# The last group's sums, norm and stores in two sequences, and the group before it at double pace

## The chip, the cores and the metric

The kernel runs on one core of a Trainium2 chip. A core has TensorE (PE in the profile), VectorE (DVE), ScalarE (ACT), GpSimd (POOL) and SyncE (SP), each with an instruction queue of its own that is worked through in order, and 16 DMA engines. The metric is the device time of one execution in microseconds; the figure quoted is the median of the runs.

## The reference, cut

32 sequences of 128 tokens with 128 features pass one decoder layer: causal self-attention (16 heads of 8), attention to a context, and a mixture of 8 experts of which every token uses 2, each followed by a residual and a layer norm.

```python
x = layernorm(x + attn(x, x, x, causal=True), ln1_g, ln1_b)
x = layernorm(x + attn(x, ctx, ctx, causal=False), ln2_g, ln2_b)
# mixture of experts
r = softmax(x @ router_w + router_b)
topw, topi = top_k(r, 2)
topw = softmax(topw)
h = gelu(x @ w1[e] + b1[e])          # for each expert e, 128 -> 512
y = h @ w2[e] + b2[e]                # 512 -> 128
x = layernorm(x + sum(topw[k] * y[topi[k]] for k in (0, 1)), ln3_g, ln3_b)
```

The layer norm is taken over the 128 features: mean, variance, `(x - m) / sqrt(v + 1e-5) * g + b`.

## The kernel before

The batch is worked in 8 groups of `G = 4` sequences, so a group is 512 tokens, held as a tile of 128 partitions by 4 by 128 (partition = token in its sequence). Both attentions of all groups come first, in half slots written out in a table. At their end each group is routed (`route`, `place`): its tokens are scattered, by expert, into rows of a DRAM buffer `xs`, and its residual (with the experts' second bias weighted in) is kept in DRAM as `x2d`.

The experts then run in two phases of four groups each (`PHASES`). A phase has 39 blocks of 128 rows (`NBL`), and each block belongs to one expert. For block i, `Pipeline.run` issues in this order:

- the load of the weights of block i + 4 (`fetch_weights`, SP's queue, 514 KB; five buffers)
- `first_layer(i)`: 4 products of 128x128 into `ph`, and four gelu activations into `h` on ScalarE (L888, L893)
- `second_layer(i - 1)`: 4 products into `po` (L904), a copy `ot<-po` on VectorE (L909), and on GpSimd a memset and an indirect DMA that scatters the 128 rows to `eo` in DRAM (L910, L911)
- in every fourth block `turn`: transposes of the rows of the next four blocks (`px`), their scatter positions (`row`, `to`) and the copy `xT<-px` on VectorE
- `beside(i)`: the hook in which the groups' final sums are advanced.

The program is under a manual schedule: each engine gets its instructions in the order in which the code issues them, and the framework only adds waits on semaphores. An instruction that waits holds up everything behind it on its engine. Scatters, gelus, copies and the final sums therefore share queues in exactly the order of the calls above.

`combine(gr)` is a generator that finishes one group. It loads `acc` (the residual from `x2d`, L977) and `gt` (both expert results of each token from `eo`, 512 KB, L979) on SP's queue, the second after the scatters of the blocks that can hold rows of the group (`needed`: 15, 23, 31 and 39 blocks of the phase). Each later call of `next` does one step:

1. the two loads
2. to 4. nothing (the load is under way)
5. `acc += wts[0] * gt[0]`, four instructions on VectorE (L996)
6. `acc += wts[1] * gt[1]`, four more
7. `bn_stats`, four (L337)
8. `bn_aggr`, four (L340), and on GpSimd `var + eps` and the power -0.5 (L341, L342)
9. a product on VectorE for the bias of the norm (L344)
10. two activations on ScalarE, which apply the norm to a sequence each (L347)
11. the other two, and on VectorE the product with the gain (L1005)
12. the addition of the bias (L1007)
13. the store of the group to the output, on SP's queue (L1009).

`step()` advances the two oldest unfinished groups by one step each, and `beside` calls it once per block. In the second phase group 4 begins in block 19, group 5 in block 27, group 6 in block 35. Group 7 needs all 39 blocks, so it begins after the loop together with what is left of groups 5 and 6. At most two groups are in `sums[:2]`, so group 7's step 1 comes when group 5 has ended. `acc` has two buffers and `gt` shares four buffers (tag `qb`).

Of the kernel before, what the change touches and what calls it, by code (L numbers as in the profile page):

```python
# [8 lines left out]
F32 = mybir.dt.float32  # L9
# [4 lines left out]
AF = mybir.ActivationFunctionType  # L14
ALU = mybir.AluOpType
AX = mybir.AxisListType

P = 128
# [5 lines left out]
G = 4  # L24
PHASES = ((0, 4), (4, 4))
NP = len(PHASES)
# [3 lines left out]
NBL = [NS + n for n in ND]  # L30
# [17 lines left out]
EPS = 1e-05  # L48
# [5 lines left out]
def bc(ap, axis, n):  # L54

    ap = ap.unsqueeze(axis)
    shape = list(ap.shape)
    shape[axis] = n
    return ap.broadcast_to(shape)
# [3 lines left out]
def kernel(  # L63
# [34 lines left out]
    nc = tc.nc  # L98
    B = x.shape[0]
    NG = B // G  # L100
# [6 lines left out]
    small = ctx.enter_context(tc.tile_pool(name="small", bufs=4))  # L107
# [6 lines left out]
    def mm_tile(shape, name, dtype=F32):  # L114
        return ps_mm.tile(shape, dtype, tag="mm", name=name)
# [36 lines left out]
    class Attn:  # L152
# [20 lines left out]
        out=hm4, in_=hm4, pattern=[[-32, RG], [-8, 4]], compare_op=ALU.is_ge,  # L173
# [3 lines left out]
        out=hm4, in_=hm4, pattern=[[32, RG], [8, 4]], compare_op=ALU.is_ge,  # L177
# [7 lines left out]
    def head_bias(a, n):  # L185

        a.bqm = const.tile([P, 4], F32, name=f"bqm{n}")
        nc.vector.tensor_scalar(a.bqm, hmask, a.bq, None, ALU.mult)
# [10 lines left out]
        out=quarter[rows], in_=quarter[rows], pattern=[[32, RG], [-1, P]],  # L199
# [4 lines left out]
        out=causal[rows], in_=causal[rows], pattern=[[32, RG], [-1, P]],  # L204
# [8 lines left out]
    def clean(t):  # L213
# [10 lines left out]
        out=mp4, in_=mp4, pattern=[[-32, RG], [-4, NPART], [-1, 4]], compare_op=ALU.is_equal,  # L224
# [10 lines left out]
    mhalf = const.tile([P, G], F32, name="mhalf")  # L235
# [14 lines left out]
    lng, lnb, lngT, lnbT, later = [], [], [], [], {}  # L250
# [78 lines left out]
    wts = const.tile([P, 2, B], F32, name="wts")  # L329
# [43 lines left out]
    PAIRS = (slice(0, 2), slice(2, 4))  # L373
# [548 lines left out]
    class Pipeline:  # L922
# [29 lines left out]
        def run(self, beside):  # L952

            self.turn()
            before = None
            for j, (k, i) in enumerate(self.all):
                self.weights(j + AHEAD)
                k.first_layer(i)
                if before:
                    before[0].second_layer(before[1])  # L960
                before = k, i
                if i % XB == min(2, k.width(i // XB) - 1):
                    self.turn()
                beside(k.ph, i)
            before[0].second_layer(before[1])


    def needed(n):

        return NS + 2 * G * (n + 1) - 1  # L970

    def combine(gr):

        p = next(p for p, (g0, n) in enumerate(PHASES) if gr.gi < g0 + n)
        first = FREE[p] + 2 * P * G * (gr.gi - PHASES[p][0])
        gr.acc = moe.tile([P, G, P], F32, tag="acc", name=f"acc_{gr.gi}")
        nc.sync.dma_start(out=gr.acc, in_=x2d[gr.gi])  # L977
        gt = act.tile([P, 2, G, 2 * P], F32, tag="qb", name=f"gt_{gr.gi}", bufs=4)[:, 0]
        i = nc.sync.dma_start(  # L979
            out=gt,  # L980
            in_=eo[p][first : first + 2 * P * G, :].rearrange(
                "(p b k) d -> p b (k d)", p=P, k=2
            ),
        )
        n = needed(gr.gi - PHASES[p][0])
        for j in phases[p].done[:n]:
            tc.add_manual_dep(i.ins, j.ins.name, SYNC, reason="results")
        for j in phases[p].done[n:]:
            tc.declare_no_dep(i.ins, j.ins, reason="rows of later groups")
        phases[p].loads.append(i)  # L990
        for _ in range(4):
            yield
        for k in range(2):
            for b in range(G):
                t = G * gr.gi + b
                nc.vector.scalar_tensor_tensor(  # L996
                    gr.acc[:, b, :], gt[:, b, P * k : P * k + P], wts[:, k, t : t + 1],
                    gr.acc[:, b, :], ALU.mult, ALU.add,
                )
            yield  # L1000
        yield from finish(gr)

    def finish(gr):
        yield from normalize(gr.acc, f"m{gr.gi}")
        nc.vector.tensor_tensor(gr.acc, gr.acc, bc(lng[2], 1, G), ALU.mult)  # L1005
        yield
        nc.vector.tensor_tensor(gr.acc, gr.acc, bc(lnb[2], 1, G), ALU.add)  # L1007
        yield
        nc.sync.dma_start(  # L1009
            out=out[G * gr.gi : G * gr.gi + G].rearrange("b p d -> p b d"), in_=gr.acc  # L1010
        )
# [82 lines left out]
    for gi in range(NG):  # L1094
# [37 lines left out]
        ph = phases[next(p for p, (g0, n) in enumerate(PHASES) if gi < g0 + n)]  # L1132
# [31 lines left out]
    def half_slot(h):  # L1164
        t, half = divmod(h, 2)
        if h < 0 and h in table:
            stir(STIR[0] if h == first_half else STIR[1])
        both_scores(unit(t), unit(t - 2), half)
        if half == 0:
            if unit(t - 3):  # L1170
                values(unit(t - 3))
            if unit(t - 1):
                maxima(unit(t - 1))
        else:
            if unit(t):
                split(unit(t))
            if unit(t - 3):
                outputs(unit(t - 3))
        for f, *args in table.pop(h, []):
            f(*args)  # L1180
        if 0 <= h < STIR[2]:
            stir(STIR[1])
# [11 lines left out]
    with tc.manual_schedule():  # L1194
        for h in range(first_half, 5):
            half_slot(h)

        for a, bo, n in ((sa, bo_s, "s"), (ca, bo_c, "c")):
            bvq = setup.tile([P, P], F32, name=f"bvq{n}")
            nc.vector.tensor_copy(bvq, a.bv.broadcast_to([P, P]))  # L1200
            pbv = mm_tile([P, P], f"pbv{n}")
            nc.tensor.matmul(pbv, lhsT=bvq, rhs=a.wo, start=True, stop=True)
            nc.vector.tensor_tensor(bo, bo, pbv, ALU.add)
        head_bias(ca, "c")
        half_slot(5)
        half_slot(6)
        lnb1c = const.tile([P, P], F32, name="lnb1c")
        nc.vector.tensor_tensor(lnb1c, lnb[0], bo_c, ALU.add)
        for h in range(7, start):
            half_slot(h)  # L1210
        left = [start]
        sums = []

        summed = {}
        for p, (g0, n) in enumerate(PHASES):
            for g in range(n):
                i = needed(g) + 4
                key = (p, i) if i < NBL[p] or p == NP - 1 else (p + 1, i - NBL[p])
                summed[key] = groups["c", g0 + g]

        def step():

            for a in sums[:2]:
                if next(a, a) is a:
                    sums.remove(a)

        def beside(ph, i):
            if table or left[0] < 2 * (len(units) + 3):
                half_slot(left[0])
                left[0] += 1  # L1230
            gr = summed.pop((ph.p, i), None)
            if gr:
                sums.append(combine(gr))
            step()

        blocks.run(beside)
        sums.extend(combine(gr) for _, gr in sorted(summed.items()))
        while sums:
            step()

# [40 lines left out]
```

## Time and profile before

| | us |
|---|---|
| median of 3 runs | 656.05 (651.39 to 667.48) |
| the profiled execution | 655.68 |
| its span, first to last instruction | 654.0 |
| TensorE busy in the span | 583.4 |
| VectorE busy | 410.7 |
| ScalarE busy | 404.4 |
| GpSimd busy | 368.6 |
| TensorE busy from 634 us on | 0.0 |

The span runs from the first to the last instruction, so the execution has 1.7 us outside it. A row of the timeline is start, length, engine, line, operation, output<-inputs, shapes, count, and in brackets the idle time of the engine before it with what ended it; "SPq" is SP's queue of issued DMAs. Neighbouring rows of one kind are merged, so a length with a count above one is that of the stretch. Instructions of one engine overlap by some hundredths of a microsecond in such rows. The number of a block is not in the rows; it follows from the order: the copies `ot<-po` of blocks 30 to 38 of the second phase start at 617.44, 621.28, 623.10, 624.88, 627.00, 628.78, 630.57, 632.41 and 633.52.

### The profile page before, as it was taken

How to read it: one execution, taken by the hardware profiler on the slowest of the kernel's cores; microseconds unless marked ns; L12 is line 12 of the kernel's file. 1: busy time of each engine (PE TensorE's matmuls, PEld its weight loads, DVE VectorE, ACT ScalarE, POOL GpSimd, SP SyncE). 2: the span in 40 equal slices, each digit the busy share in tenths (PEclk: the TensorE clock that was granted, in tenths of full speed). 3: DMA queues.
4: the chain of work that ended last, by engine and by line, in shares of the span. 5: the costliest groups of instructions: out<-in, count | busy, mean ns of one | idle time of the engine just before them, and what ended most of it. 6: DMA issues, size and time to landing. Idle time of an engine off the chain costs nothing. (4 is left out here: it accounts for less than half of the span.)

```text
span 654.0 us, 22743 instructions
## 1 busy us (share of the span) xinstructions
PE 583.4 (89%) x9247; PEld 497.4 (76%) x9247; DVE 410.7 (63%) x1327; ACT 404.4 (62%) x919; POOL 368.6 (56%) x749
## 2 busy tenths in 40 slices
PE   8999899999998999999999988988897978999870
PEld 7777787878876777777876866777797878998870
DVE  3345456665667766786787778884867634543563
ACT  4266576787677468667758676645674446665652
POOL 3256465544645557538737525633788885664561
PEclk9599899999999899999999999987999979999995
DMA  6110610832010011001001100422897989999972
GB/s 130 35 35 4 122 43 3 244 136 66 4 34 3 11 47 32 3 7 56 10 20 34 35 4 14 167 71 73 264 285 261 351 306 365 375 344 383 349 254 70
DMA packets 48041, 82.53 MB, mean 126 GB/s; under 512 B 7968, under 2 KB 26464, under 8 KB 47936
## 3 DMA queue, kind: packets, MB, share of 16 engines
q1 hardware_dynamic: 42816, 71.57, 34.3%
q0 software_dynamic: 4544, 9.38, 3.9%
q8 instruction: 72, 1.18, 0.7%
q14 instruction: 33, 0.27, 0.1%
q10 hardware_dynamic: 576, 0.13, 0.1%
HBM read 62.15 MB, written 23.10 MB: 130 GB/s over the span
## 5 line engine op out<-in xcount | busy, mean ns | idle before, releaser
L893 ACT ACTIVATE h<-ph,wd 128x128 f32<-128x128 f32 x312 | 88.7, 369 | 63.3 <-PE ph L888 21.3
L487 DVE TENSOR_REDUCE m_s<-sc_s 128x8 f32<-128x1024 f32 x64 | 78.3, 1223 | 76.6 <-PE sc_s L448 75.6
L499 POOL TENSOR_SCALAR_AFFINE_SELECT pr_s<-pr_s 128x1024 f32<-128x1024 f32 x64 | 69.9, 1092 | 84.4 <-ACT pr_s L495 84.1
L911 POOL DMA_INDIRECT eo<-ot,to x78 | 77.8, 997 | 55.2 <-DVE acc L996 13.5
L495 ACT ACTIVATE pr_c<-st_c 128x1024 f32<-128x1024 f32 x64 | 65.9, 1029 | 60.7 <-PE st_c L460 60.7
L487 DVE TENSOR_REDUCE m_c<-sc_c 128x8 f32<-128x1024 f32 x64 | 78.1, 1220 | 31.0 <-PE sc_c L448 19.5
L888 PE MATMUL ph<-xT,wd 128*128 128x128 f32 x624 | 86.7, 284 | 9.9 <-DMA wd<-wpk 5.2
L495 ACT ACTIVATE pr_s<-st_s 128x1024 f32<-128x1024 f32 x64 | 65.8, 1028 | 42.9 <-PE st_s L460 42.2
L888 PEld LDWEIGHTS ph<-xT,wd 128*128 128x128 f32 x624 | 78.3, 197 | 14.7 <-DMA wd<-wpk 4.1
L904 PE MATMUL po<-wd,h 128*128 128x128 f32 x624 | 84.6, 280 | 4.9 <-ACT h L893 4.9
L904 PEld LDWEIGHTS po<-wd,h 128*128 128x128 f32 x624 | 77.9, 195 | 5.5 <-ACT h L893 5.5
L448 PE MATMUL sc_c<-k_c,qb_c 32*128 32x128 f32 x1024 | 75.5, 286 | 6.7 <-DVE m_c L487 5.1
L448 PE MATMUL sc_s<-k_s,qb_s 32*128 32x128 f32 x1024 | 76.2, 289 | 0.0
L448 PEld LDWEIGHTS sc_c<-k_c,qb_c 32*128 32x128 f32 x1024 | 63.2, 189 | 12.4 <-DVE m_c L487 7.8
L460 PE MATMUL st_c<-qb_c,k_c 32*128 32x128 f32 x1024 | 71.7, 279 | 0.0
L784 POOL DMA_INDIRECT xs<-x,slots x64 | 64.3, 1005 | 12.8 <-issue 12.2
L460 PE MATMUL st_s<-qb_s,k_s 32*128 32x128 f32 x1024 | 71.6, 278 | 0.0
L460 PEld LDWEIGHTS st_s<-qb_s,k_s 32*128 32x128 f32 x1024 | 67.0, 190 | 0.9
L460 PEld LDWEIGHTS st_c<-qb_c,k_c 32*128 32x128 f32 x1024 | 67.3, 191 | 0.2
L448 PEld LDWEIGHTS sc_s<-k_s,qb_s 32*128 32x128 f32 x1024 | 66.9, 198 | 0.3 <-issue 0.2
L909 DVE COPY ot<-po 128x128 f32<-128x128 f32 x78 | 22.5, 290 | 63.8 <-PE po L904 56.7
L442 PE MATMUL sc_s<-causal,quarter 32*128 32x512 bf16 (+3 forms) x512 | 48.4, 309 | 4.2 <-DVE m_s L487 4.0
(247 smaller groups left out, 1202.8 us busy)
## 6 DMA issues: line engine op xcount, KB each, us to landing
wd<-wpk SPq DMA_DIRECT2D x78, 514.0 KB, 5.4
xs<-blank SPq DMA_DIRECT2D x2, 2600.0 KB
xt<-xs SPq DMA_DIRECT2D x20, 260.0 KB, 6.0
wpk<-in_L_xattn_e_w_dram SPq DMA_DIRECT2D x16, 256.0 KB, 9.5
gt<-eo SPq DMA_DIRECT2D x8, 512.0 KB, 7.0
xg<-in_x_dram SPq DMA_DIRECT2D x8, 256.0 KB, 4.8
eg<-in_ctx_dram SPq DMA_DIRECT2D x8, 256.0 KB
x2d<-base SPq DMA_DIRECT2D x8, 256.0 KB
```

What stands on the lines that cost most here:

```text
L442: nc.tensor.matmul(sc[:, i, :, k], lhsT=quarter[rowsof(g), j, :], rhs=bc(causal[rowsof(g), j, k], 1, 4), start=j == 0, stop=False,)
L448: nc.tensor.matmul(sc[:, i, r, :], lhsT=new.group.qb[rowsof(g), new.b, r, :], rhs=new.group.k[rowsof(g), new.b, :], start=not new.masked, ...
L460: nc.tensor.matmul(st[:, i, r, :], lhsT=old.group.k[rowsof(g), old.b, :], rhs=old.group.qb[rowsof(g), old.b, r, :], start=False, stop=r == 3,)
L487: nc.vector.tensor_reduce(new.m[:, 8 * half : 8 * half + 8], sc.rearrange("p i r k -> p (i r) k"), AX.X, ALU.max,)
L495: nc.scalar.activation(old.pr[:, hs, :], st.rearrange("p i r k -> p (i r) k"), AF.Exp, scale=SCALE)
L499: nc.gpsimd.affine_select(out=old.pr[:, hs, :], in_=old.pr[:, hs, :], pattern=[[0, 8], [1, P]], compare_op=ALU.is_ge, fill=0.0, base=0, ch ...
L784: i = nc.gpsimd.indirect_dma_start(out=xs[ph.p][:, :], out_offset=bass.IndirectOffsetOnAxis(ap=slots[:, k, t : t + 1], axis=0), in_=gr.x2[ ...
L888: nc.tensor.matmul(hid[:, c, :], lhsT=w[:, c * P : (c + 1) * P], rhs=self.xT[i // XB][:, i % XB, :], start=True, stop=True,)
L893: nc.scalar.activation(self.h[i][:, c, :], hid[:, c, :], AF.Gelu, bias=w[:, B1 + c : B1 + c + 1])
L904: nc.tensor.matmul(po, lhsT=h[:, c, :], rhs=w[:, W2 + c * P : W2 + (c + 1) * P], start=c == 0, stop=c == NFC - 1,)
L909: nc.vector.tensor_copy(ot, po)
L911: s = nc.gpsimd.indirect_dma_start(out=eo[p][:, :], out_offset=bass.IndirectOffsetOnAxis(ap=self.to[q][:, i % XB : i % XB + 1], axis=0), i ...
```

## The change

In the last eight blocks of the second phase (i from 31 to 38) `beside` calls `step()` twice. Groups 5 and 6 so take two steps per block there: group 5 does steps 5 to 12 in blocks 31 to 34 and stores in block 35 before group 6's loads are issued in the same block; group 6 does steps 1 to 8 in blocks 35 to 38. Group 6's steps 5 and 6 thereby stand between the copies of blocks 36 and 37, its steps 7 and 8 between those of 37 and 38.

After the loop the last group's loads are issued first, then the remaining steps of group 6, then the last group alone. For it `combine` skips the empty steps and calls `last_sums`. That splits the four sequences in two pairs. For each pair VectorE does the sums and statistics sequence by sequence and GpSimd the power; then VectorE's product and ScalarE's activations pair by pair; then gain and bias pair by pair on tiles of 128x256. Each pair has its own store, the first on SP's queue and the second on ScalarE's.

```diff
--- before.py
+++ after.py
@@ -969,6 +969,45 @@
 
         return NS + 2 * G * (n + 1) - 1
 
+    def last_sums(gr, gt):
+
+        rs = [small.tile([P, 2, 2], F32, tag="rs", name=f"rs_l{ab.start}") for ab in PAIRS]
+        for n, ab in enumerate(PAIRS):
+            st = small.tile([P, 2, 6], F32, tag="st", name=f"st_l{n}")
+            mv = small.tile([P, 2, 2], F32, tag="mv", name=f"mv_l{n}")
+            for b in range(2):
+                y, t = gr.acc[:, ab.start + b, :], G * gr.gi + ab.start + b
+                for k in range(2):
+                    nc.vector.scalar_tensor_tensor(
+                        y, gt[:, ab.start + b, P * k : P * k + P], wts[:, k, t : t + 1], y,
+                        ALU.mult, ALU.add,
+                    )
+                nc.vector.bn_stats(st[:, b, :], y)
+            for b in range(2):
+                nc.vector.bn_aggr(mv[:, b, :], st[:, b, :])
+            nc.gpsimd.tensor_scalar(rs[n][:, 0], mv[:, :, 1], EPS, None, ALU.add)
+            nc.gpsimd.tensor_tensor(rs[n][:, 0], rs[n][:, 0], mhalf[:, :2], ALU.pow)
+            rs[n] = rs[n], mv
+        for n, ab in enumerate(PAIRS):
+            r, mv = rs[n]
+            y = gr.acc[:, ab]
+            nc.vector.scalar_tensor_tensor(
+                r[:, 1], mv[:, :, 0], -1.0, r[:, 0], ALU.mult, ALU.mult
+            )
+            for b in range(2):
+                nc.scalar.activation(
+                    y[:, b, :], y[:, b, :], AF.Identity,
+                    bias=r[:, 1, b : b + 1], scale=r[:, 0, b : b + 1],
+                )
+        for n, ab in enumerate(PAIRS):
+            y = gr.acc[:, ab]
+            nc.vector.tensor_tensor(y, y, bc(lng[2], 1, 2), ALU.mult)
+            nc.vector.tensor_tensor(y, y, bc(lnb[2], 1, 2), ALU.add)
+            (nc.sync, nc.scalar)[n].dma_start(
+                out=out[G * gr.gi + ab.start : G * gr.gi + ab.stop].rearrange("b p d -> p b d"),
+                in_=y,
+            )
+
     def combine(gr):
 
         p = next(p for p, (g0, n) in enumerate(PHASES) if gr.gi < g0 + n)
@@ -988,6 +1027,10 @@
         for j in phases[p].done[n:]:
             tc.declare_no_dep(i.ins, j.ins, reason="rows of later groups")
         phases[p].loads.append(i)
+        if gr.gi == NG - 1:
+            yield
+            last_sums(gr, gt)
+            return
         for _ in range(4):
             yield
         for k in range(2):
@@ -1232,9 +1275,16 @@
             if gr:
                 sums.append(combine(gr))
             step()
-
+            if ph.p == NP - 1 and i >= ph_last - 8:
+                step()
+
+        ph_last = NBL[-1]
         blocks.run(beside)
-        sums.extend(combine(gr) for _, gr in sorted(summed.items()))
+        (last,) = (combine(gr) for gr in summed.values())
+        next(last)
+        while sums:
+            step()
+        sums.append(last)
         while sums:
             step()
```

## Prediction

> **What bounds the kernel now.** I read the chain of waits first, from 612 us to the end, because the change only touches what is issued after block 31 of the last phase. Its columns are start, length and what.
>
> ```profile
> 612.15 6.93 DMA wd<-wpk
> ...
> 631.42 2.07 PE po L904 x16
> ...
> 634.44 2.26 DMA eo<-ot,to
> ...
> 636.90 2.69 DMA gt<-eo
> ...
> 649.13 0.70 DVE acc L1005
> 649.84 0.02 issue
> 649.86 0.69 DVE acc L1007
> ```
>
> Until 633.5 TensorE and the weight loads set the pace. Then comes a chain in which nothing overlaps: copy of block 38 (633.52), its scatter (634.44), the load of group 7's rows (636.90), sums, norm, store, end at 654.0. That is 20.5 us, all that the second half of the change can shorten. Next, SP's own timeline, for who loads and stores when:
>
> ```profile
> 625.26 0.43 SPq L977 DMA_DIRECT2D acc<-x2d  x1
> 626.00 0.33 SPq L979 DMA_DIRECT2D gt<-eo  x1
> 633.37 0.39 SPq L1009 DMA_DIRECT2D out_dram<-acc  x1
> 635.72 0.32 SPq L977 DMA_DIRECT2D acc<-x2d  x1
> 636.90 0.32 SPq L979 DMA_DIRECT2D gt<-eo  x1
> 644.68 6.33 SPq L1009 DMA_DIRECT2D out_dram<-acc  x2
> ```
>
> The first two rows are group 6's loads, the third is group 5's store, then group 7's loads, then two stores (the last at 650.6). In order of time, VectorE and GpSimd around the end of the blocks:
>
> ```profile
> 630.57 0.29 DVE L909 COPY ot<-po 128x128 f32<-128x128 f32 x1 [1.49 <-PE po L904]
> ...
> 632.41 0.29 DVE L909 COPY ot<-po 128x128 f32<-128x128 f32 x1
> ...
> 632.98 1.15 POOL L911 DMA_INDIRECT eo<-ot,to  x1 [0.80 <-DVE ot L909]
> ...
> 633.52 0.29 DVE L909 COPY ot<-po 128x128 f32<-128x128 f32 x1 [0.22 <-PE po L904]
> 633.73 2.18 DVE L996 SCALAR_TENSOR_TENSOR acc<-gt,wts,acc 128x128 f32<-128x128 f32 x8
> ...
> 634.44 0.99 POOL L911 DMA_INDIRECT eo<-ot,to  x1 [0.22 <-DVE acc L996]
> ...
> 641.22 1.14 DVE L996 SCALAR_TENSOR_TENSOR acc<-gt,wts,acc 128x128 f32<-128x128 f32 x4 [2.53 <-DMA gt<-eo]
> ```
>
> The three copies are blocks 36, 37 and 38. Group 6's sums (the row of eight) stand behind the last copy: whatever they wait for delays no scatter. Group 7's rows, asked for at 636.90, reach VectorE at 641.22, 4.3 us later on almost idle DMA engines. On the page the same load takes 7.0 us at the median, in the stream of weights.
>
> **The change, part by part.** I write ot_b for the copy of block b.
>
> *Group 5 at double pace (blocks 31 to 34).* Its eight sums move to block 31, where VectorE idled 2.37 us before ot_31 (621.28): free. Statistics follow ot_31, done about 622.7. GpSimd does the add and power (0.23 and 1.04) right after block 31's scatter (ends 622.92), so to 624.3, ahead of block 32's scatter, which slips about 0.9 us; group 6's load needs blocks 0 to 30 only, so nobody waits. VectorE's 0.16 us product follows at 624.35, and ScalarE's first two activations run 624.55 to 625.4 *ahead* of block 34's gelu (it was 624.04). A pair takes 0.78 before the next instruction, the four gelus 1.03: that gelu starts 625.33, and its quarters end at 625.7, 625.95, 626.2, 626.5; TensorE's second layer needs them at 625.9, 626.1, 626.35, 626.55. That is a cover of 0.1 to 0.2 us, so I cost it at nothing; without cover it would be up to 1.3 us. The other two activations end 627.25; product with gain and addition (0.69 each) end at 628.7. ot_34 slips from 627.00 to 628.75 and ot_35 to 629.0, hidden by the four PSUM buffers; ot_36 is on time at 630.57.
>
> *SP's queue.* Group 5's store, formerly after everything, is now issued in front of group 6's two loads, and it waits for the addition above. Store at 628.75, acc load at 629.2, gt load (0.74 us behind it, as in the rows above) at **629.9** instead of 626.00.
>
> *Group 6 at double pace.* Its sums now stand directly behind ot_36 and in front of ot_37. They are ready to run at 630.9 but their rows were asked for only 1 us before. Nearest row: group 7's load, on nearly idle DMA engines with one acc load ahead: 4.3 us. By then the weight queue has drained (last weights issued at 625.2). So the rows are there at **634.2**; the far end is the 7.0 us of the page, 636.9; the near end is 632.5, where the old load landed (626.00 plus 6.5, the fastest in the DMA view). VectorE stands still 3.3 us, and ot_37 stands behind the wait.
>
> Here a rule must be weighed. The Trainium skill, "DMA: Bandwidth & Descriptors", section "Anatomy of one DMA", prices a GpSimd-issued transfer at 2.0 us plus bytes over 436 GB/s; for 512 KB this estimate is 3.2 us, so rows at 633.1. The same page, "Rules for kernel authors", says to issue early and wait late, which speaks against this change: it halves the blocks between load and use. The row says 4.3 us for this very transfer; the sum below would be 1.1 us lower by the rule. I take the row.
>
> *What queues behind.* Eight sums 634.2 to 636.4; ot_37 to 636.7 (block 37's matmuls were done near 632.2); statistics and aggregates 0.86 and 0.36, to 637.8; ot_38 to 638.1. GpSimd: scatter 37 from 637.0 to 638.1; then group 6's add and power, now placed *ahead* of the last scatter, to 639.5; memset; scatter 38 at **639.75** instead of 634.44: 5.3 us late. Of these 3.3 are the stall, the rest the group's own VectorE and GpSimd work, which formerly ran while scatter and load were in flight. Group 7's rows are asked for at 642.2 and arrive at 646.5. Group 6's norm, its 1.65 us of activations, its product and addition (to 642.9) now lie in that load's shadow: this takes 1.37 us of VectorE out of the final stretch. acc of group 7 is no longer held by group 5's store (it was, until 635.72), but that was not the last thing waited for.
>
> *Last group in two sequences.* From arrival, using rows of 0.34 (sum), 0.28 (statistics), 0.15 (aggregate), and 0.04 between dependent instructions (649.13 + 0.69 to 649.86): one tile takes 0.34 + 0.04 + 0.34 + 0.04 + 0.28 = 1.04, two overlapped by 0.08 are 2.0, with the aggregates 2.19; the second pair ends at 4.31. GpSimd starts 0.16 later (645.83 after 645.67) and takes 1.35: 5.82. Product 0.16: 6.0. Two activations 0.89: 6.97. Product and addition on 128x256: not in the trace; between 0.35 (half of 0.69) and 0.55 (the 128x384 copy); the step from the copy of 384 to that of 512 elements, 0.13 per 128, gives 0.42. Addition ends at 7.88, second store issued at 7.92. The first half's activations, product, addition and store end before this. Old: 641.22 to 650.60 is 9.38. Saved: **1.46**. Last store: 256 KB took 2.5 us (650.6 to 653.1); ScalarE's 64 KB load at the start took 2.2; the half-size store on ScalarE's queue I put at 2.3, saved 0.2 (nothing to 0.4, the latter if SP's issue of 0.39 is all hidden; nothing stands behind it on ScalarE).
>
> **Sum.** +5.3 − 1.5 − 0.2 = **+3.6 us**. The profiled execution took 655.68 (span 654.0 and 1.7 around it): 659.3 by it. The median of the three runs is 656.05, 0.4 higher, so I forecast **659.5**: about half a per cent slower, within the 2% which is about what a measurement of this kernel can tell from no change.
>
> **Rivals.**
> 1. *The rows come in time* (ends not slower). If group 6's rows are there when ot_36 is done, VectorE does not stop: sums to 633.1, ot_37, statistics to 634.5, ot_38 to 634.8, GpSimd's power to 636.1, scatter 38 at 636.3, 1.9 late, less 1.7: 655.9 by the profiled execution, so 656.3, no change. For: the old load was in VectorE's hands no later than 633.7. Against: it would need store 5 to leave by 625.5, and its addition comes 3 us later. It decides from a load in hand before 631. Chance 0.15.
> 2. *The load keeps its median of 7.0 us* because store, acc and gt (1 MB) share the engines: rows at 636.9, all after it 2.7 later: 662.2, slower by 0.9%. It decides from rows later than about 635.5. For: 6.5 to 7.5 in every landing listed. Against: these all lay behind 514 KB weight loads. Chance 0.22.
> 3. *The double pace does stop TensorE*: ScalarE's gelu of blocks 34 and 35 late by more than its cover. Then about 1.3 us is added before the stall, but the stall swallows it where it delays only ot_37; at most 660.8. For: cover of only 0.1 us. Against: only two gelus are behind it. Chance 0.10.
>
> The forecast itself has 0.53. **Range**: mechanisms reach from 656 to 662. The three runs before lie at 651.39, 656.05 and 667.48, so a median of few runs moves by several us without any cause in the kernel; I take 3 us below and 4 above: 653 to 666. Chances: over 2% faster (below 643) nothing in the cases gives, 0.01 for scatter; over 2% slower (above 669) likewise only scatter on top of rival 2: 0.05; within: 0.94.
>
> **What would show it.** In the timeline after: store 5 in front of group 6's loads near 628.8; gt of group 6 near 630; VectorE idle some 3 us before the first of group 6's sums, put down to the gt load, between ot_36 and ot_37; ot_37 and ot_38 near 636.5 and 638; last scatter near 639.8; last gt load near 642; from its arrival to the second store near 7.9 us instead of 9.4. The forecast is wrong if VectorE doesn't idle there (rival 1), if the last scatter is before 637, or if the last stretch is not shorter.

## The result and the profile after

The changed kernel takes 658.61 us at the median of 22 runs (654.37 to 664.63), against 655.36 of the kernel before in 22 runs on the same chip (649.88 to 667.48). The ratio is **1.0048, 95% interval 1.0026 to 1.007**, which is 3.2 us (0.0048 times 655.4): slightly slower, and within 2% of no change. The ratio leaves out runs over 1.5% above the fastest of their kernel. The profiled execution took 662.31 us with a span of 659.5 (before: 655.68 and 654.0).

The two spans differ by 5.5 us, but the copy of block 36, `ot_36`, starts at 630.57 before and at 632.66 after, and this lag of 2.1 us does not come from the change: the copy of block 30, ahead of the first block that the change touches, is already 2.4 late (619.84 against 617.44). I therefore measure **from the start of `ot_36` to the end of the span**, and call this the last stretch. It is 654.0 − 630.57 = 23.43 us before and 659.5 − 632.66 = 26.84 after: 3.41 longer. What happens in blocks 31 to 35 lies outside it; from the copy of block 30 to `ot_36` it is 12.82 us after and 13.13 before. The first evidence is the chain of waits after the change (start, length, what):

```profile
631.69 5.36 DMA gt<-eo
...
637.14 1.21 DVE acc L1039 x5
...
641.36 1.05 POOL rs_m L342
...
642.63 2.36 DMA eo<-ot,to
...
645.20 3.70 DMA gt<-eo
```

Before, the chain at this place went from TensorE's last products to the last scatter (634.44). Now it goes through a load of group 6's rows, group 6's sums, and even group 6's power on GpSimd, before it comes to the last scatter at 642.63. SP's timeline shows why that load is there:

```profile
630.44 0.40 SPq L1052 DMA_DIRECT2D out_dram<-acc  x1
630.94 0.45 SPq L1016 DMA_DIRECT2D acc<-x2d  x1
631.69 0.32 SPq L1018 DMA_DIRECT2D gt<-eo  x1
632.97 0.32 SPq L1016 DMA_DIRECT2D acc<-x2d  x1
645.20 0.32 SPq L1018 DMA_DIRECT2D gt<-eo  x1
645.80 0.39 SPq L1052 DMA_DIRECT2D out_dram<-acc  x1
655.60 0.39 SPq L1006 DMA_DIRECT2D out_dram<-acc  x1
```

The first row is group 5's store. SP waited 3.4 us for group 5's addition (L1050) before it, and for nothing between it and group 6's two loads, which stand behind it at 630.94 and 631.69. Measured from `ot_36`, the second is issued 0.97 us ahead of it, where it was 4.57 ahead (626.00). In VectorE's timeline the wait stands in the brackets (idle time, and what ended it):

```profile
632.66 0.29 DVE L909 COPY ot<-po 128x128 f32<-128x128 f32 x1 [1.50 <-PE po L904]
637.14 2.19 DVE L1039 SCALAR_TENSOR_TENSOR acc<-gt,wts,acc 128x128 f32<-128x128 f32 x8 [4.18 <-DMA gt<-eo]
639.25 0.28 DVE L909 COPY ot<-po 128x128 f32<-128x128 f32 x1
...
640.50 0.26 DVE L909 COPY ot<-po 128x128 f32<-128x128 f32 x1
...
648.98 0.74 DVE L981 SCALAR_TENSOR_TENSOR acc<-gt,wts,acc 128x128 f32<-128x128 f32 x2 [3.25 <-DMA gt<-eo]
```

After block 36 VectorE stands still for 4.18 us for group 6's rows, with the copies of blocks 37 and 38 queued behind the wait. GpSimd's timeline has the second delay, the power ahead of the last scatter:

```profile
641.36 1.04 POOL L342 TENSOR_TENSOR rs_m<-rs_m,mhalf 128x4 f32<-128x4 f32 x1
642.37 0.09 POOL L910 MEMSET apart<- 1x1 f32 x1
642.63 1.10 POOL L911 DMA_INDIRECT eo<-ot,to  x1 [0.17 <-DVE rs_m L344]
```

The last of all stores is issued on ScalarE's queue:

```profile
656.65 0.41 ACTq L1006 DMA_DIRECT2D out_dram<-acc  x1
```

The last stretch, cut into its four parts ("rows" are the last group's):

| part of the last stretch, us | before | after | difference | forecast |
|---|---|---|---|---|
| `ot_36` to the issue of the last `gt` load | 6.33 | 12.54 | +6.21 | +5.3 |
| that issue to the first use of its rows | 4.32 | 3.78 | −0.54 | 0 |
| first use to the last store's issue | 9.38 | 7.67 | −1.71 | −1.46 |
| last store's issue to the end | 3.40 | 2.85 | −0.55 | −0.2 |
| sum | 23.43 | 26.84 | +3.41 | +3.6 |

### The profile page after: what moved, and what is told of

The parts are those of the page before. It is cut to its first block, busy times and chain, and to the rows that moved or that the text cites. A ratio compares the mean times of both kernels' runs of the same rounds, so it can differ in the third digit from the quotient of the medians.

```text
span 659.5 us, 22753 instructions
## 1 busy us (share of the span) xinstructions
PE 581.5 (88%) x9247; PEld 495.4 (75%) x9247; DVE 412.3 (63%) x1330; ACT 404.4 (61%) x919; POOL 368.9 (56%) x751
## 3 DMA queue, kind: packets, MB, share of 16 engines
q0 software_dynamic: 4544, 9.38, 3.9%
## 5 line engine op out<-in xcount | busy, mean ns | idle before, releaser
L448 PE MATMUL sc_s<-k_s,qb_s 32*128 32x128 f32 x1024 | 74.8, 285 | 0.0
L448 PEld LDWEIGHTS sc_s<-k_s,qb_s 32*128 32x128 f32 x1024 | 65.5, 194 | 0.3 <-issue 0.2
```

The costliest lines, as they stand in the source:

```text
L448: nc.tensor.matmul(sc[:, i, r, :], lhsT=new.group.qb[rowsof(g), new.b, r, :], rhs=new.group.k[rowsof(g), new.b, :], start=not new.masked, ...
```

## The experiments

They ran on three slower chips, on which the kernel before takes 680 to 682 us at the median. Each ratio is against the kernel before on the same chip. The last stretch is compared with the 23.43 and 26.84 us of the first two profiles, since the kernel before has no profile of these chips here. A stretch is that of one profiled execution; where the ratio's interval holds 1, the runs do not tell the kernel from the one before, whatever the stretch. The edits are against the changed kernel where nothing else is said.

**1. The two sequences alone.** No double pace.

```diff
             step()
-            if ph.p == NP - 1 and i >= ph_last - 8:
-                step()
...
         (last,) = (combine(gr) for gr in summed.values())
+        step()
         next(last)
```

> The last group in two sequences, but one step per block as before. I read the stretch from the start of the copy of block 36 to the end of the span: before 23.4 us (630.57 to 654.0), after 26.8 us (632.66 to 659.5). Theory A (the loss is VectorE's wait for group 6's rows in front of the last two copies, plus group 6's own work in front of the last scatter; the two sequences are a gain): no wait here, the last scatter 3.9 us after the copy of block 36 as before; group 6's gain and bias (1.4 us) end about 0.6 us after the last rows arrive and hold the last sums by that; the last sums to the last store 7.7 us, the store 2.9: stretch 21.7, 1.7 us less than before, ratio 0.997. Rival C (the two sequences with their dependent instructions are themselves the loss): 23.4 or more, ratio 1.00 or above.

The ratio is **0.9955 (0.9927 to 0.9982)**; the last stretch is 668.5 − 647.02 = 21.48 us, 1.95 shorter than before. In VectorE's timeline no copy waits for rows, and the last sums (L981) follow group 6's gain and bias without a gap:

```profile
649.75 0.29 DVE L909 COPY ot<-po 128x128 f32<-128x128 f32 x1 [0.28 <-PE po L904]
649.95 2.18 DVE L1039 SCALAR_TENSOR_TENSOR acc<-gt,wts,acc 128x128 f32<-128x128 f32 x8
...
657.35 0.69 DVE L1050 TENSOR_TENSOR acc<-acc,lnb 128x512 f32<-128x512 f32 x1
657.96 0.73 DVE L981 SCALAR_TENSOR_TENSOR acc<-gt,wts,acc 128x128 f32<-128x128 f32 x2
```

This half of the change is a gain over the kernel before, and it is the version to take. It was not run beside the changed kernel on one chip; the changed kernel's interval begins at 1.0026 on the first chip and at 0.9977 in experiment 10.

**2. The double pace alone**, with the last group worked whole as before.

```diff
-        if gr.gi == NG - 1:
-            yield
-            last_sums(gr, gt)
-            return
         for _ in range(4):
             yield
```

> The double pace and the order of the changed kernel, but the last group summed, normed and stored in the old way, whole. Theory A: VectorE idle about 4 us in front of group 6's sums as in the changed kernel, last rows at VectorE 16.3 us after the copy of block 36; then the old sequence, with nothing of group 6 between, about 8.1 us, and the whole store 3.4: stretch 27.8, 4.4 us more than before, ratio 1.006 to 1.007. Of the 1.7 us that the last stretch of the changed kernel became shorter, 1.3 then belongs to group 6's work having left it and 0.4 to the two sequences. Rival C: 23.4, ratio 1.00.

The ratio is **1.006 (1.0032 to 1.0089)**, the last stretch 675.3 − 648.36 = 26.94: 3.51 longer than before. So the loss lies in this half. VectorE's timeline has the same wait as the changed kernel:

```profile
651.70 2.19 DVE L1035 SCALAR_TENSOR_TENSOR acc<-gt,wts,acc 128x128 f32<-128x128 f32 x8 [3.05 <-DMA gt<-eo]
...
663.82 2.19 DVE L1035 SCALAR_TENSOR_TENSOR acc<-gt,wts,acc 128x128 f32<-128x128 f32 x8 [3.53 <-DMA gt<-eo]
...
671.23 0.69 DVE L1046 TENSOR_TENSOR acc<-acc,lnb 128x512 f32<-128x512 f32 x1
```

It also splits the gain at the end. From the arrival of the last rows (663.82) to the end of the last addition (671.92) are 8.1 us without the two sequences; before it was 9.3 (641.22 to 650.55), since group 6's gain and bias lay in between, and with the sequences it is 7.6 (648.98 to 656.57). So of the 1.7 us, about 1.2 come from group 6 being out of the way and only 0.5 from the overlap.

**3. Group 6's loads ahead of group 5's store**, in block 35; all else as changed.

```diff
                 sums.append(combine(gr))
+                if ph.p == NP - 1 and i == 35:
+                    next(sums[1])
+                    next(sums[0], None)
+                    next(sums[1])
+                    sums.pop(0)
+                    return
             step()
```

> The changed kernel, but in block 35 group 6's two loads are issued in front of group 5's store instead of behind it. Stretches are read from the start of the copy of block 36 to the end of the span: 23.4 us before, 26.8 changed. Theory A (part of VectorE's wait is made on SP's queue, where the loads stand behind a store that waits for an addition): the gt load is issued 4.5 to 5 us ahead of the copy of block 36 instead of 1 us, lands 6.5 us later among the weights, VectorE waits 1.2 to 2.0 us instead of 4.2, stretch 24.0 to 24.8, ratio 1.001 to 1.002. Rival D (the wait is only that two blocks are too short for the load, the store in front of it costs nothing): wait 3.5 us or more, stretch 26 or more, ratio 1.005.

The ratio is 1.0004 (0.9977 to 1.003), the last stretch 674.7 − 651.58 = 23.12, shorter than expected. In SP's timeline the residual's load is issued at 645.90, 5.7 us ahead of `ot_36` (it was 1.7 ahead), and the store follows at 648.30. VectorE's wait is all but gone:

```profile
651.58 0.29 DVE L909 COPY ot<-po 128x128 f32<-128x128 f32 x1 [1.80 <-PE po L904]
652.08 2.23 DVE L1039 SCALAR_TENSOR_TENSOR acc<-gt,wts,acc 128x128 f32<-128x128 f32 x8 [0.21 <-DMA gt<-eo]
```

Experiment 6, on the same chip, keeps the changed order on SP's queue and waits 1.74 us, with TensorE as long from `ot_33` to `ot_36` (7.08 us; 7.06 here). One swap thus takes away nearly the whole wait. It went further than expected because the load was shorter: the rows' load was issued at 646.92, 4.7 us ahead of `ot_36` as expected, but took 5.2 us instead of 6.5. In the changed kernel TensorE took only 5.99 us for the same blocks; at that pace an estimated 1.3 us of wait (0.21 plus 7.06 − 5.99) would be left.

**4. Group 6's loads two blocks earlier** (block 33), its steps 5 on where the change has them.

```diff
-        for _ in range(4):
+        for _ in range(8 if gr.gi == NG - 2 else 4):
             yield
...
-                i = needed(g) + 4
+                i = needed(g) + 4 - 2 * (p == NP - 1 and g == 2)
```

> The changed kernel, with group 6's two loads issued two blocks earlier (block 33 instead of 35, behind the weights of block 37 and in front of those of block 38 and of group 5's store); its sums stay where the change put them. Theory A: the rows are there when VectorE reaches the sums (idle below 0.6 us instead of 4.2), the last scatter about 6 us after the copy of block 36 instead of 10, stretch 22.7 to 23.3 instead of 26.8, ratio 0.998 to 1.000. Rival B (the loss is the place of group 6's sums, statistics and power in front of the last scatter, the wait being only time that would have passed anyway): stretch 25.5 or more, ratio 1.003 or more. If the weights of block 38 come late through it, TensorE idles in front of block 38's first layer, and the stretch keeps up to 1 us of it.

The ratio is 1.0003 (0.9971 to 1.0035), the last stretch 678.1 − 654.59 = 23.51. VectorE goes from `ot_36` to the sums without a wait:

```profile
654.59 0.29 DVE L909 COPY ot<-po 128x128 f32<-128x128 f32 x1 [1.50 <-PE po L904]
654.80 2.18 DVE L1039 SCALAR_TENSOR_TENSOR acc<-gt,wts,acc 128x128 f32<-128x128 f32 x8
657.58 0.29 DVE L909 COPY ot<-po 128x128 f32<-128x128 f32 x1 [0.60 <-PE po L904]
```

This is the prediction's first rival made real, and it gives that rival's time: no loss and no gain. In part that is luck. TensorE stood 0.94 us in front of block 38's first layer, which the rival did not have, and the shorter end saved more than the rival counted. The bracket of that wait says only "issue" here, but in experiment 5, with the same loads, TensorE's row at this place names block 38's weights, which are now issued behind them:

```profile
650.77 1.16 PE L888 MATMUL ph<-xT,wd 128*128 128x128 f32 x8 [1.09 <-DMA wd<-wpk]
```

**5. As 4, and a single step in block 38**, so that group 6's aggregates, add and power stand behind the last copy and scatter.

```diff
-            if ph.p == NP - 1 and i >= ph_last - 8:
+            if ph.p == NP - 1 and ph_last - 8 <= i < ph_last - 1:
                 step()
```

> As the kernel with the loads two blocks earlier, and in block 38 one step instead of two, so that group 6's aggregates and its power on GpSimd come behind the last copy and the last scatter. Theory A: no wait, the last scatter 4.0 to 4.8 us after the copy of block 36, group 6 finished before the last rows arrive, then 7.7 and 2.9 us: stretch 20.9 to 21.6, about 2 us less than before, ratio 0.996 to 0.998; it would beat both kernels. Rival B says the same of the order but keeps the wait as harmless: it expects the gain over the kernel with the early loads alone to be 4 us or more.

The last stretch is 671.2 − 649.72 = 21.48, 2.03 shorter than in 4 and as short as in 1. The ratio, 0.9981 (0.9945 to 1.0018), does not tell it from no change.

**6. The changed kernel with a single step in block 38**, the edit of 5 alone.

> The changed kernel, but one step instead of two in block 38, so that group 6's aggregates and its power on GpSimd come behind the last copy and the last scatter; loads and wait as in the changed kernel. Theory A: VectorE still waits about 4 us, the last scatter comes 1.4 to 1.7 us earlier (8.3 to 8.6 us after the copy of block 36), the stretch is 25.1 to 25.5, ratio 1.002 to 1.004. Rival B (the order on GpSimd is harmless, because the scatter would have been held up by the one before it): stretch 26.5 or more.

The last stretch is 678.7 − 656.16 = 22.54, far below what I expected, and the ratio 1.0 (0.9961 to 1.0039). Two things are mixed: the wait was only 1.74 us, and the power has moved. (Of the 2.44 us of wait that are missing against the first profile, 1.1 are that `ot_36` came later after group 6's loads, the rest that the rows arrived sooner after their issue.) The second can be read alone, as the time from group 6's first sum to the last scatter. GpSimd's timeline:

```profile
662.12 0.96 POOL L911 DMA_INDIRECT eo<-ot,to  x1 [0.21 <-issue]
663.11 0.24 POOL L341 TENSOR_SCALAR rs_m<-mv_m 128x4 f32<-128x4 f32 x1
```

The first sum started at 658.19, so this is 3.93 us; it is 5.49 in the changed kernel (637.14 to 642.63), and 5.49 and 5.53 in experiments 2 and 3. The place of the aggregates, the add and the power therefore costs **1.56 us** of the last scatter's time.

**7. Group 6's gain and bias out of the way.** In experiment 1 the last sums stand 1.4 us behind these two instructions. Here they are issued later, between the two pairs' small products, where VectorE waits for GpSimd. The edit stands on that of experiment 1; its lines that only split the generator and hand it over are left out here.

```diff
                 nc.scalar.activation(
                     y[:, b, :], y[:, b, :], AF.Identity,
                     bias=r[:, 1, b : b + 1], scale=r[:, 0, b : b + 1],
                 )
+            for _ in rest:
+                pass
...
-        while sums:
-            step()
+        groups["c", NG - 1].rest = sums.pop()
+        for _ in range(6):
+            next(groups["c", NG - 1].rest)
         sums.append(last)
```

> The last group in two sequences with one step per block, and group 6's gain and bias on VectorE (1.4 us) moved from in front of the last sums into the gap in which VectorE waits for the second power. Theory A: the last sums start when the last rows arrive (about 10.0 us after the copy of block 36; with the two sequences alone they started 10.9 us after it), the second product slips by 0.2 to 0.4 us, stretch 20.6 to 20.9 against 21.5 with the two sequences alone, ratio 0.994 to 0.995; it would be the fastest so far. Rival: the gap is shorter than the moved work by more than 0.4 us, or group 6's store meets the last ones: 21.3 or more.

The last stretch is 672.1 − 650.82 = 21.28, 0.4 longer than expected and only 0.2 shorter than in experiment 1; the ratio is 0.9999 (0.9971 to 1.0027). The last sums did begin on arrival of the rows (660.78, 9.96 us behind `ot_36`; in experiment 1 it is 10.94). But GpSimd's timeline shows its second pair slowed:

```profile
663.19 0.23 POOL L988 TENSOR_SCALAR rs_l<-mv_l 128x2 f32<-128x2 f32 x1 [4.92 <-DVE mv_l L987]
663.50 0.72 POOL L989 TENSOR_TENSOR rs_l<-rs_l,mhalf 128x2 f32<-128x2 f32 x1
665.32 0.56 POOL L988 TENSOR_SCALAR rs_l<-mv_l 128x2 f32<-128x2 f32 x1 [1.10 <-DVE rs_l L994]
665.97 1.14 POOL L989 TENSOR_TENSOR rs_l<-rs_l,mhalf 128x2 f32<-128x2 f32 x1
```

VectorE ran the moved instructions beside the second pair, at 665.12 and 665.85 for 0.69 each. The same add and power took 0.23 and 0.72 for the first pair; beside them they took 0.56 and 1.14, 0.75 more in all, which ate most of what the edit freed.

**8. As 7, with both last stores on SP's queue.**

```diff
-            (nc.sync, nc.scalar)[n].dma_start(
+            nc.sync.dma_start(
```

> As the kernel with the two sequences and group 6's gain and bias in the gap, but both of the last stores on SP's queue instead of one on SP's and one on ScalarE's. Theory A (the last store is short because it is half as large, the second queue is worth little): the second store's issue begins within 0.1 us as early, since the first issue (0.4 us) ended half a microsecond before; end of span within 0.2 us of that kernel, ratio within 0.001 of it. Rival E (the second queue is what shortened the end by 0.55 us): 0.4 us or more later.

The ratio is 0.9966 (0.9937 to 0.9996), 0.0033 below that of experiment 7 where 0.001 was expected. The two intervals overlap, and nothing in the last stretch accounts for such a gap, so ratios on these chips may differ by some thousandths without a cause at the end of the program. The profiled execution took 684.79 us against a median of 677.60, so only a distance within it is used: SP's last store, issued near 680.25, ended with the span at 683.1, 2.85 us later. ScalarE's store takes 2.87 in experiment 7 (669.23 to 672.1) and 2.85 in the changed kernel. So the second queue does not show in the end; what remains as the likely reason is the smaller store.

**9. As 1, with group 6's gain and bias on GpSimd.**

```diff
-        nc.vector.tensor_tensor(gr.acc, gr.acc, bc(lng[2], 1, G), ALU.mult)
+        eng = nc.gpsimd if gr.gi == NG - 2 else nc.vector
+        eng.tensor_tensor(gr.acc, gr.acc, bc(lng[2], 1, G), ALU.mult)
         yield
-        nc.vector.tensor_tensor(gr.acc, gr.acc, bc(lnb[2], 1, G), ALU.add)
+        eng.tensor_tensor(gr.acc, gr.acc, bc(lnb[2], 1, G), ALU.add)
```

> The last group in two sequences with one step per block, and group 6's gain and bias (128x512) on GpSimd instead of VectorE, in front of the last group's powers. GpSimd does such a product in 1.28 us when VectorE runs beside it elsewhere in the trace, so both are done about 2.6 us after group 6's activations, more than 1 us ahead of the first power of the last group. Theory A: VectorE takes the last rows as they arrive, 10.0 us after the copy of block 36, then 7.7 us to the last store and 2.9: stretch 20.5 to 20.8 us (21.5 with the two sequences alone, 23.4 before), ratio 0.994 to 0.996. Rival F (VectorE and GpSimd slow each other, as where group 6's products on VectorE stood beside a power that took 1.14 instead of 0.72 us): VectorE's sums beside GpSimd's products take over 20% longer, or the second power is late; 21.3 or more.

The ratio is 0.9958 (0.9931 to 0.9986), the last stretch 677.4 − 654.94 = 22.46, longer than expected and than in experiment 1. VectorE's first two sums, then GpSimd's two products:

```profile
665.25 2.39 DVE L981 SCALAR_TENSOR_TENSOR acc<-gt,wts,acc 128x128 f32<-128x128 f32 x2 [2.12 <-DMA gt<-eo]
```

```profile
664.89 1.26 POOL L1049 TENSOR_TENSOR acc<-acc,lng 128x512 f32<-128x512 f32 x1 [1.97 <-ACT acc L347]
666.23 1.26 POOL L1051 TENSOR_TENSOR acc<-acc,lnb 128x512 f32<-128x512 f32 x1
```

The two sums take 0.74 in the changed kernel and 2.39 here: VectorE lost 1.65 us beside GpSimd's products, more than the 1.4 us that they were to save it.

**10. The changed kernel once more**, on the chip of experiment 9.

> The changed kernel as it is, for the same chip as the other experiments. Theory A: VectorE idle 2 to 4.5 us in front of group 6's first sum (the longer the sooner TensorE gets to block 36), from that sum to the start of the last scatter 5.5 us, from the last load's arrival to the second store 7.7 us, ratio 1.003 to 1.006. If the stretch is below 24 us, the wait is not a property of the change but of one profiled execution.

The ratio is 1.0009 (0.9977 to 1.0041): inconclusive, since it allows both no loss and most of the loss found first. The last stretch is 683.3 − 658.18 = 25.12, still longer than before's 23.43. VectorE's timeline:

```profile
660.66 2.19 DVE L1039 SCALAR_TENSOR_TENSOR acc<-gt,wts,acc 128x128 f32<-128x128 f32 x8 [2.18 <-DMA gt<-eo]
...
672.73 0.74 DVE L981 SCALAR_TENSOR_TENSOR acc<-gt,wts,acc 128x128 f32<-128x128 f32 x2 [3.48 <-DMA gt<-eo]
```

The mechanism is the same, its size is not: the wait is 2.18 instead of 4.18. All the rest of the stretch (5.48 from the first sum to the last scatter, 7.68 from the last rows' use to the last store) is as in the first profile. In the four executions with SP's order as changed (the changed kernel twice, 2 and 6) the wait was 4.18, 3.05, 2.18 and 1.74. It is the difference between two things that move on their own, the rows' arrival and TensorE's arrival at block 36. The residual's load, issued just ahead of the rows', shows both:

| | residual's load ahead of `ot_36` | from that load to the first use of the rows | wait |
|---|---|---|---|
| changed kernel | 1.72 | 6.20 | 4.18 |
| experiment 2 | 2.74 | 6.08 | 3.05 |
| experiment 10 | 2.78 | 5.26 | 2.18 |
| experiment 6 | 2.81 | 4.84 | 1.74 |

In all four, group 5's store, the two residuals' loads and three scatters were issued within 2.2 us of the rows' load. Its arrival still moves by 1.4 us, and no run shows why.

## Why the prediction was right

**SP's order: right.** The store of group 5 is the first in the queue, and the load of group 6's rows comes 1.25 us behind it (1.15 by the forecast). Experiment 3 keeps the pace and turns this order round: the wait falls from 1.74 us (experiment 6, same chip) to 0.21.

**The load's length: the term that was too small in this profile.** I took 4.3 us, from a load on almost idle DMA engines. From issue to first use it took 5.45 (631.69 to 637.14). The load was issued 0.3 us earlier against `ot_36` than worked out (0.97 ahead instead of 0.67), so the stall was 4.18 instead of 3.3. The engines were not idle. The table of stretches (duration, busy time of PE, PEld, DVE, ACT and POOL, clock, DMA share, GB/s) of the changed kernel shows it:

```profile
632.00:634.00 2.00, 2.00 (x20) 2.00 (x19) 0.29 (x1) 1.36 (x6) 1.68 (x3) 1.00 1.04 257
634.00:636.00 2.00, 1.31 (x12) 1.11 (x10) 0.00 (x0) 0.74 (x3) 0.41 (x2) 1.00 0.77 257
...
647.00:649.00 2.00, 0.00 (x0) 0.00 (x0) 0.02 (x1) 0.00 (x0) 0.00 (x0) 0.50 0.91 283
```

While group 6's rows came in, the share was 1.04; the store of group 5 and two residual loads of 256 KB each were issued within 2.6 us around it, and scatters ran too. That this sharing made the load long is not shown. The last load (third row) had company as well, since group 6's store of 256 KB was issued 0.6 us behind it (645.80), and it took 3.78; in experiment 7, with no store issued within 3 us of it, it took 4.08. And the table under experiment 10 has the rows arrive up to 1.4 us sooner with the same transfers around them. So the cause of the 5.45 stays open, and the forecast's 4.3 was not a bad figure for this load, only for this execution. The price in the Trainium skill, "DMA: Bandwidth & Descriptors", section "Anatomy of one DMA", is for transfers issued by GpSimd, and its estimate of 3.2 us is further off: this load is issued by SP, and no load of such rows that VectorE waited for was in use less than 3.5 us after its issue.

**What queues behind it: right.** From the first sum to the last scatter I worked out 5.55 us, and it is 5.49. Experiment 6 shows that 1.56 of these are the place of group 6's aggregates, add and power alone, nearly half of the net loss.

**The last group's load: 0.54 too long.** I left it at 4.3 us, and it took 3.78.

**The last group's work: right in kind, the saving 0.25 too small.** The power of a pair (128x2) took 0.73 us, not the 1.04 of the row on 128x4 that I used. The product on 128x256 took 0.42, as derived.

**The last store: the saving too small.** I gave it 0.2 us and it was 0.55. I had compared with a load at the start of the program; the row of the kernel before, issue to end of span, was nearer.

**TensorE's cover: open.** From `ot_33` to `ot_36` it took 5.99 us against 5.69, a loss of up to 0.3 where I had put 0. Experiments with double pace took 5.69 to 7.08 and those with single pace 6.13 to 6.21. TensorE's rows name late weights for part of the long ones (0.32 us in experiment 2, 0.17 in 6) and no cause for the rest, so the pace's own share can't be read.

**The rivals.** Rows in time needs an earlier load, and experiment 4 shows its time. Rows after 7.0 us did not come true, though the truth, 5.4, lies between it and the forecast.

That the sum (+3.4 against +3.6) came out closer than its terms is partly luck: the stall was 0.9 too small and the savings 1.1 too small, and these cancel. It is also one pair of profiles: in experiment 10 the last stretch was only 1.7 us longer than before, mainly because the wait was shorter by 2.0.

## What to carry to other kernels

Before work is drawn forward in an in-order queue, ask what it will wait for and who stands behind it: here eight sums drawn forward by two blocks held two copies, their scatters and the last load. If a group's store waits for late work, issue the next group's loads ahead of it (1.74 us of wait became 0.21 here), and keep slow side work (here a power of 1 us) behind the scatter that others wait for. Splitting a final chain into two sequences was worth having, about 1 us with its smaller last store, and clearing other work out of the end brought as much again (about 1.2).

## What the runs showed of the hardware

**VectorE and GpSimd hold each other up.** Experiment 7 has GpSimd's small operations grow from 0.23 to 0.56 and from 0.72 to 1.14 us beside VectorE's products of two tiles, and experiment 9 has two VectorE sums grow from 0.74 to 2.39 beside GpSimd's products. The Trainium skill, "SBUF — State Buffer", section "SBUF: two separate sides", gives a reason: the two share a pair of ports, and whichever starts first, a VectorE operation with two inputs from SBUF or a GpSimd operation that reads SBUF, holds the pair for the whole instruction while the other waits. The rows agree in kind: in experiment 7 the add ended at 665.88, just after VectorE's product (665.81). So idle time on one of the two was not free room for such work of the other.

**A power on GpSimd has a large fixed part**: it took 0.72 us for 128x2 and 1.04 for 128x4, so half the columns save 30%. A straight line through these two, which is an estimate, has 0.40 us at no columns.

**The end of the program was longer with a larger last store**: 2.85 us from its issue to the end of the span for 128 KB, on either queue, and 3.3 to 3.4 for 256 KB (experiment 2 and the kernel before).

**The same load, among the same transfers, does not take the same time**: group 6's rows were in use 4.84 to 6.20 us after their residual's load was issued, in four executions with the same order on SP's queue.
